# Cross-attention with a routed FFN on one core: scatters spread over half slots, x and result laid out by group and token, the last layernorm and the blocks' weights moved in the ending

## The chip, the cores and the metric

The kernel runs on one core of a Trainium2 chip. The metric is device time in microseconds for one launch. The engines are PE (TensorE), ACT (ScalarE), DVE (VectorE), POOL (GpSimd) and SP (SyncE, which here only issues DMAs). Each engine works through its own instructions in order.

## The reference, cut to what matters

There are 64 batches of 128 tokens with 128 features, and 77 context rows of 96 features for each batch. Everything is fp32.

```python
x = x + xattn(layernorm(x), ctx)       # 16 heads of 64, softmax over 77 keys, w_out, b_out
x2 = layernorm(x)
logits = x2 @ router_w.T               # 8 experts
gate = logits of the 2 experts with the highest softmax(logits), 0 elsewhere
moe = sum_e gate[:, e] * ((silu(x2 @ w1[e].T) * (x2 @ w3[e].T)) @ w2[e].T)      # I = 176
moe = moe + (silu(x2 @ sw1.T) * (x2 @ sw3.T)) @ sw2.T                          # shared expert
return x + moe
```

## The kernel before, in words

**Groups, units, half slots.** The batches are cut into 16 groups of four (G = 4). An attention unit is one batch with half of the heads, so there are 128 units, eight to a group. The main loop (lines 1075 to 1092) walks the units; each has two half slots, `run(2k)` and `run(2k+1)`, at which steps of a plan are called. A group thus has 16 half slots, group g starts at half slot 16 g, and `end` is 256. The plan is a dictionary written by `at(when, steps)` (lines 841 to 956). Each step puts its instructions behind those already there on each engine; the framework then places the instructions and their waits, and the order on POOL in particular can differ a little from the order of the plan.

**Attention.** Queries are never formed: keys times folded weights (pk, L334, copied to kx by ACT, L341) meet the transposed x (ps, L351). DVE subtracts the maximum (sc, L362), ACT takes exp (L366), DVE sums and inverts (ri, L375), POOL scales (tile `at`, L381 to L385, two buffers), PE transposes (pa, L420), ACT copies (aT, L423), PE multiplies with folded values (py, L430; the values are pv, L403, copied to vo by ACT, L408), and DVE adds to the residual x1 (L431). The group's inputs are loaded by SP two groups ahead (`load_inputs`, x at L111).

**Layernorm and router.** In the next group's half slots the finished group is normalised: DVE takes the statistics, POOL computes rs (L279), DVE the shift (L287), ACT writes the normalised rows into `pay` (L291, one buffer), PE transposes them (pxT, L304), ACT copies to x2T (L305), PE computes the logits, DVE chooses two experts and finds each token's row. `send(c, b)` (L632) is an indirect DMA on POOL (L635): it scatters the 128 rows of batch b for choice c, each with its destination and its gate, into a DRAM buffer `sent`, sorted by expert. There are eight sends to a group, and `pay` can be written again when the eight have been done.

**Blocks.** The groups form three sets (9, 5 and 2 groups). When the rows of a set are sent, `tables` (L675) turns the counts into a table of blocks of 128 rows of one expert. A `Quad` is four such blocks: `load` (L736, SP) reads the rows, `weights` (L758) copies the four experts' weights within SBUF, two by ACT and two by DVE, `transpose` (L764, L766), `first` and `rest` (L771) make the hidden rows in two parts, `down` (L783, L784) multiplies with w2, ACT scales by the gate into y (L791, two buffers), and `answer(j)` (L793) is an indirect DMA on POOL (L795), four to a quad, that scatters the results to a DRAM buffer by token. Set 0 has 20 quads, spread over the attention of set 1's groups; set 1 has 12, of which seven run every two half slots over the last attention and five (KEPT) in the ending.

**Combining.** `Combine` reloads a group's residual (L818) and its answers (L821), adds (L830), and stores the result (L834). For all groups but the last two the residual had been parked in DRAM.

**The ending.** After the last unit, a list of jobs (the kept quads, the two remaining shared experts, and the last set's quads) is run in a software pipeline (`ending`, L1020 to L1035). `ahead_of[k]` holds the steps that are issued before job k's `first`, `within[k]` those behind it. The last group's layernorm is split: batches 0 to 2 (`most_of`) are normalised in the last half slots of the plan, batch 3 (`rest_of`) at the start of the ending. The quads' copies of weights stand in `ahead_of`, two jobs early.

The places that the change touches:

```python
nc.sync.dma_start(out=xg, in_=x[bs].rearrange("b t d -> t b d"))                       # L111
at(p + 9 + k, lambda g=g, c=c, b=k: routers[g].send(c, b))                             # L926
at(p + 5 + j // 2, lambda quad=quad, j=j: quad.answer(j))                              # L950
at(end - 1, last("transpose", most_of), last("logits", most_of))                       # L990
0: [last("stats", rest_of), last("normed", rest_of)],                                  # L993
ahead_of.setdefault(max(k - 2, 5 if k > KEPT + 1 else 0), []).append(job["weights"])   # L1003
```

Of the kernel before, what the change touches and what calls it, by code (L numbers as in the profile page):

```python
# [8 lines left out]
F32 = mybir.dt.float32  # L9
# [6 lines left out]
B, NQ, D = 64, 128, 128  # L16
# [15 lines left out]
G = 4  # L32
NG = B // G
# [3 lines left out]
KEPT = 5  # L37
# [23 lines left out]
def xattn_moe_kernel(  # L61
# [17 lines left out]
    nc = tc.nc  # L79
# [26 lines left out]
    def load_inputs(g):  # L106
        bs = slice(g * G, (g + 1) * G)
        cT = grp.tile([DC, G, NKV], F32, tag="cT", name=f"cT_{g}", bufs=2)
        nc.sync.dma_start(out=cT, in_=ctxT[:, bs, :])
        xg = grp.tile([128, G, D], F32, tag="xg", name=f"xg_{g}", bufs=2)  # L110
        nc.sync.dma_start(out=xg, in_=x[bs].rearrange("b t d -> t b d"))  # L111
        return xg, cT

    def load_first_keys(g):
# [12 lines left out]
    def load_last_keys(g):  # L127
# [3 lines left out]
        return cR  # L131

    inputs, transposed = {0: load_inputs(0)}, {0: load_transposed(0)}
    first_keys, last_keys = {0: load_first_keys(0)}, {0: load_last_keys(0)}
    for q in range(2):
# [11 lines left out]
    def load_expert(e):  # L147
        nc.sync.dma_start(out=wx_sb[:, e, :], in_=wx[e * 128 : (e + 1) * 128, :])
# [11 lines left out]
    for i in range(NAT):  # L160
        a = const.tile([128, 8 * (KM + KS)], F32, name=f"at_{i}")
# [643 lines left out]
    class Combine:  # L805
# [24 lines left out]
                nc.vector.tensor_tensor(self.x1, self.x1, self.answers[:, c], ALU.add)  # L830

        def store(self):
            g = self.g
            self.queue.dma_start(out=out[g * G : (g + 1) * G].rearrange("b t d -> t b d"), in_=self.x1)  # L834

# [3 lines left out]
    def at(when, *steps):  # L841
        plan.setdefault(when, []).extend(steps)

    atts = {}
    routers = {}
# [26 lines left out]
    def load_group(g):  # L872
        inputs[g] = load_inputs(g)
# [10 lines left out]
    for g in range(NG):  # L884
        p = 16 * g
# [15 lines left out]
    def route(g, step, *args):  # L901
        if g not in routers:
            routers[g] = Router(g, next(s for s in sets if s.start <= g < s.start + s.n), atts[g].x1)
        getattr(routers[g], step)(*args)

    def routing(g, p, *steps):
        for k, step in steps:
            at(p + k, lambda step=step: route(g, step))

    g = 0  # L910
# [4 lines left out]
    for g in range(NG - 1):  # L915
        p = 16 * (g + 1)
        routing(g, p, (0, "stats"), (1, "normed"), (3, "transpose"), (3, "twice"), (4, "logits"), (4, "exps"), (5, "choose"), (6, "choose_second"))
    for st in sets:
        for g in range(st.start, min(st.start + st.n, NG - 1)):
            p = 16 * (g + 1)  # L920
            routing(g, p, (8, "place"))
            if g < NG - 2:
                routing(g, p, (11, "shared_up"), (12, "shared_rest"), (14, "shared_down"), (17, "park"))
            for k in range(4):
                for c in range(2):
                    at(p + 9 + k, lambda g=g, c=c, b=k: routers[g].send(c, b))  # L926
    end = 16 * NG
    for st in sets[:-1]:
        p = 16 * (st.start + st.n)
# [2 lines left out]
        st.ready = p + 16  # L932
    for g in range(2, 2 + E):
        at(16 * g + 8, lambda e=g - 2: load_expert(e))
    kept = []
    for st, after in zip(sets, sets[1:]):
        quads = [Quad(st, q) for q in range(st.quads)]
        until = after.ready - 16 if after is not sets[-1] else end - 4
        if after is sets[-1]:
            quads, kept = quads[:-KEPT], quads[-KEPT:]  # L940
        for q, quad in enumerate(quads):
            p = st.ready + (until - st.ready) * q // (len(quads) - 1)
            at(p - 3, quad.load)
            at(p - 1, quad.weights)
            at(p, quad.transpose)
            at(p + 1, quad.first)
            at(p + 2, quad.rest)
            at(p + 4, quad.down)
            for j in range(QUAD):
                at(p + 5 + j // 2, lambda quad=quad, j=j: quad.answer(j))  # L950
        if after is not sets[-1]:
            for j in range(st.n):
                c = Combine(st, j)
                at(p + 7 + 2 * j, c.load)
                at(p + 9 + 2 * j, c.add)
                at(p + 10 + 2 * j, c.store)
# [16 lines left out]
    def last(step, *args):  # L973
        return lambda: route(NG - 1, step, *args)
# [3 lines left out]
    def shared(g):  # L978
        return {
            "first": lambda: route(g, "shared_up", True),  # L980
            "rest": lambda: route(g, "shared_rest", True),
            "down": lambda: route(g, "shared_down"),
        }

    jobs = blocks[:3] + [shared(NG - 2)] + blocks[3:KEPT] + [shared(NG - 1)] + blocks[KEPT:]

    most_of, rest_of = range(G - 1), range(G - 1, G)
    at(end - 3, last("stats", most_of))
    at(end - 2, last("normed", most_of))
    at(end - 1, last("transpose", most_of), last("logits", most_of))  # L990

    ahead_of = {
        0: [last("stats", rest_of), last("normed", rest_of)],  # L993
        1: [last("choose"), last("choose_second")],
        2: [last("place"), last("twice")] + [last("send", c, b) for b in range(G) for c in range(2)],
        4: [lambda: tables(last_set)],
    }

    within = {0: [last("transpose", rest_of), last("logits", rest_of), last("exps")]}
    for k, job in enumerate(jobs):  # L1000

        if k and "weights" in job:
            ahead_of.setdefault(max(k - 2, 5 if k > KEPT + 1 else 0), []).append(job["weights"])  # L1003

    def ahead(k, step):
        ahead_of.setdefault(k, []).append(step)
# [1 line left out]
    for j in range(before_last.n):  # L1008
        c = Combine(before_last, j)
        k = KEPT + 3 + j  # L1010
# [3 lines left out]
    for j, queue in zip(range(last_set.n), (nc.sync, nc.scalar)):  # L1014
        c = Combine(last_set, j, queue, routers)
# [4 lines left out]
    def ending():  # L1020
        def do(k, step):
            if 0 <= k < len(jobs):
                jobs[k].get(step, lambda: None)()

        for k in range(max(ahead_of) + 1):
            do(k + 2, "load")
            for step in ahead_of.get(k, ()):
                step()
            do(k, "first")
            for step in within.get(k, ()):  # L1030
                step()
            do(k + 1, "transpose")
            do(k, "rest")
            do(k - 1, "down")
            do(k - 1, "answer")  # L1035
# [3 lines left out]
    at(end - 2, jobs[0]["weights"])  # L1039
    at(end - 1, jobs[0]["transpose"])  # L1040
    at(end + 2, ending)

    def run(when):
# [3 lines left out]
    def unit(k):  # L1047
        g, b, t = units[k]
        return attention_of(g), b, t
# [25 lines left out]
    for k in range(len(units) + 1):  # L1075
# [3 lines left out]
        if k and k % 2 == 0:  # L1079
            a, b, t = unit(k - 1)  # L1080
# [4 lines left out]
        a, b, t = unit(k)  # L1085
# [11 lines left out]
    last = {}  # L1097
# [12 lines left out]
def _laid_out(inputs):  # L1110

    import numpy as np

    a = {k: np.asarray(v) for k, v in inputs.items()}
    f = np.float32

    def packed(w1, w3, w2):

        w = np.zeros((128, WALL), f)
        w[:, W1:W3] = w1[:128].T  # L1120
        w[:, W3:WR] = w3[:128].T
        w[:, WR : WR + IR] = w1[128:].T
        w[:, WR + 64 : W2F] = w3[128:].T
        w[:, W2F:W2R] = w2[:, :128].T
        w[:IR, W2R:] = w2[:, 128:].T
        return w

    keys = a["ctx_768"].transpose(2, 0, 1)
    ctxR = np.zeros((DC, B, KS), f)
    ctxR[:, :, :KR] = keys[:, :, KM:]  # L1130
    ctxM = keys[:, :, :KM].reshape(DC, B // 2, 2 * KM)
    ctxM = np.concatenate([ctxM, ctxM[:, :, :KM]], axis=2)

    def by_pair(w):

        return w.reshape(NH // 2, 128, -1).transpose(1, 0, 2)

    w1, w2, w3 = (a[f"L0_ffn_w{n}"] for n in (1, 2, 3))
    return {
        "x": a["x"],  # L1140
        "xT": a["x"].transpose(2, 0, 1),
        "ctxT": keys,
        "ctxM": ctxM,
        "ctxR": ctxR,
        "wqT": by_pair(a["L0_xattn_w_q"].T),
        "wkT": by_pair(a["L0_xattn_w_kv"][:, :INNER].T),
        "wvT": by_pair(a["L0_xattn_w_kv"][:, INNER:].T),
        "w_out": by_pair(a["L0_xattn_w_out"]),
        "b_out": a["L0_xattn_b_out"],
        "rwT": a["L0_ffn_router_w"].T,  # L1150
        "wx": np.concatenate([packed(w1[e], w3[e], w2[e]) for e in range(E)]),
        "wsh": packed(a["L0_ffn_sw1"], a["L0_ffn_sw3"], a["L0_ffn_sw2"]),
    }
# [19 lines left out]
```

## Time and profile before

| | |
|---|---|
| time, median of 3 runs | 1010.59 us (1010.37 to 1012.74) |
| profiled execution, its own time | 1054.01 us |
| its span | 1052.3 us |
| its mean granted TensorE clock | 0.956 |
| PE busy | 945.9 us, 90% |
| DVE busy | 677.8 us, 64% |
| ACT busy | 653.7 us, 62% |
| POOL busy | 521.1 us, 50% |
| sends (L635) | 128 of 992 ns |
| answers (L795) | 152 of 986 ns |
| DMA packets | 81410, of them 63392 of 512 B to 2 KB |

The profile is of one execution, which took longer than the runs that were timed without it. A busy PE is not a PE at its peak, and busy shares are means over very different stages: the attention of the first nine groups, the attention with blocks between its units, and the ending. A row of the timeline has the start, the duration, the engine, the line, the operation, what is written from what, and how often; the brackets give the engine's idle time before it and what ended it. The suffix `_f` is the layernorm ahead of the FFN, `_a` that ahead of the attention.

### The profile page before, as it was taken

To read this page: it belongs to the slowest core of one execution; us is meant where nothing else is said; L and a number is where in the kernel's file an instruction comes from. 1 tells how busy PE (TensorE), PEld (TensorE's weight loads), DVE (VectorE), ACT (ScalarE), POOL (GpSimd) and SP (SyncE) were. 2 spreads that over 40 slices of the span, in tenths; PEclk is the share of its full clock that TensorE was granted. 3 is DMA by queue.
4 is the path that set the end of the run, shared out by engine and by line. 5 is a ranking of instruction groups with operands and counts; after the bars stand their busy time and mean duration, and the time that the engine had idled before them with its cause. 6 is when DMAs were issued, how large, how long until landed. Compare 5 with 4: busy or idle time off the path is not lost. (4 is left out here: it accounts for less than half of the span.)

```text
span 1052.3 us, 18905 instructions
## 1 busy us (share of the span) xinstructions
PE 945.9 (90%) x6136; PEld 785.1 (75%) x6136; DVE 677.8 (64%) x1773; ACT 653.7 (62%) x1421; POOL 521.1 (50%) x692
## 2 busy tenths in 40 slices
PE   7999999999999999999899898799999887666781
PEld 6887887878787787868787687698787676564781
DVE  4667767676676677786676567466758778334342
ACT  4777767667676766757667557557676475433550
POOL 3345363653536456353645555553656426626353
PEclk9999999999999999999999899999999899878896
DMA  5212122122212311233123122222212653211364
GB/s 169 75 39 79 57 62 79 56 72 76 76 40 63 99 55 55 83 85 88 47 77 91 56 67 60 60 66 84 64 57 90 195 169 108 64 28 58 89 199 138
DMA packets 81410, 86.16 MB, mean 82 GB/s; under 512 B 11424, under 2 KB 63392, under 8 KB 81312
## 3 DMA queue, kind: packets, MB, share of 16 engines
q1 hardware_dynamic: 66352, 56.29, 19.3%
q0 software_dynamic: 8960, 18.50, 5.3%
q10 hardware_dynamic: 6000, 10.16, 2.7%
q8 instruction: 49, 0.80, 0.3%
q14 instruction: 49, 0.40, 0.1%
HBM read 48.38 MB, written 36.53 MB: 81 GB/s over the span
## 5 line engine op out<-in xcount | busy, mean ns | idle before, releaser
L334 PEld LDWEIGHTS pk<-cT,wkq_sb 96*128 96x128 f32 x1024 | 159.4, 191 | 71.3 <-issue 47.9
L795 POOL DMA_INDIRECT answers<-y,to x152 | 149.9, 986 | 114.9 <-ACT y L791 52.7
L341 ACT COPY kx<-pk 128x308 f32<-128x308 f32 x256 | 104.1, 416 | 145.1 <-PE pk L334 103.9
L334 PE MATMUL pk<-cT,wkq_sb 96*128 96x154 f32 x1024 | 177.1, 297 | 1.3 <-DVE wkq_sb L246 1.3
L351 PE MATMUL ps<-kx,xgT 128*128 128x308 f32 x512 | 161.7, 437 | 10.1 <-DVE sc L362 9.5
L430 PEld LDWEIGHTS py<-vo,aT 128*128 128x128 f32 x1280 | 158.5, 197 | 15.4 <-ACT vo L408 2.7
L430 PE MATMUL py<-vo,aT 128*128 128x128 f32 x1280 | 160.7, 281 | 3.7 <-ACT aT L423 2.3
L383 POOL TENSOR_TENSOR at<-sc,ri 128x512 f32<-128x512 f32 x64 | 67.1, 1049 | 192.2 <-DVE ri L375 148.1
L635 POOL DMA_INDIRECT sent<-pay,row x128 | 126.9, 992 | 62.6 <-DVE part L625 29.4
L408 ACT COPY vo<-pv 64x512 f32<-64x512 f32 x256 | 147.0, 574 | 3.0 <-remote 0.7
L403 PE MATMUL pv<-wvo_sb,cM 96*128 96x512 f32 x256 | 131.5, 595 | 3.0 <-DVE hr L505 1.2
L373 DVE TENSOR_REDUCE sm<-sc 128x8 f32<-128x616 f32 x128 | 101.2, 790 | 39.6 <-ACT sc L366 38.7
L366 ACT ACTIVATE sc<-sc,rs_a 128x616 f32<-128x616 f32 x128 | 104.8, 819 | 31.1 <-DVE sc L362 30.2
L423 ACT COPY aT<-pa 128x512 f32<-128x512 f32 (+1 forms) x256 | 96.2, 429 | 42.3 <-PE pa L420 25.8
L351 PEld LDWEIGHTS ps<-kx,xgT 128*128 128x128 f32 x512 | 91.2, 194 | 38.5 <-issue 9.5
L381 POOL TENSOR_TENSOR at<-sc,ri 128x256 f32<-128x256 f32 x128 | 76.6, 621 | 87.1 <-DVE ri L375 41.8
L362 DVE TENSOR_TENSOR sc<-ps,mx 128x616 f32<-128x616 f32 x128 | 102.4, 800 | 12.6 <-POOL at L383 0.5
L360 DVE TENSOR_REDUCE mx<-ps 128x8 f32<-128x616 f32 x128 | 98.4, 768 | 8.7 <-PE ps L351 7.0
L420 PE MATMUL pa<-ident,at 128*128 128x128 f32 x640 | 92.0, 274 | 2.2 <-DVE lg L546 1.3
L771 PE MATMUL p<-xT,w 128*128 128x128 f32 x608 | 76.8, 280 | 14.0 <-ACT xT L766 7.3
L771 PEld LDWEIGHTS p<-xT,w 128*128 128x128 f32 x608 | 72.9, 196 | 18.2 <-ACT xT L766 9.3
L420 PEld LDWEIGHTS pa<-ident,at 128*128 128x128 f32 x640 | 75.2, 142 | 13.4 <-issue 11.8
(147 smaller groups left out, 1430.6 us busy)
## 6 DMA issues: line engine op xcount, KB each, us to landing
xb<-sent SPq DMA_DIRECT2D x152, 65.0 KB
last_values<-vn ACTq DMA_DIRECT2D x32, 256.0 KB
vo<-last_values SPq DMA_DIRECT2D x64, 128.0 KB
ya<-answers SPq DMA_DIRECT2D x15, 512.0 KB
xg<-in_x_dram SPq DMA_DIRECT2D x16, 256.0 KB
xgT<-in_xT_dram SPq DMA_DIRECT2D x16, 256.0 KB
parked<-x SPq DMA_DIRECT2D x14, 256.0 KB
ya<-parked SPq DMA_DIRECT2D x14, 256.0 KB
```

Source lines behind the costliest of these rows:

```text
L334: nc.tensor.matmul(pk[:, k].rearrange("p (b k) -> p b k", k=NKV), wkq_sb[:, 2 * i + k, :], self.cT[:, 2 * p : 2 * (p + 1), :], start=True, ...
L341: nc.scalar.copy(self.kx[p][:, hs, :], pk)
L351: nc.tensor.matmul(ps[:, r, : 4 * NKV].rearrange("p (j k) -> p j k", k=NKV), self.xgT[:, ts], self.kx[p][:, h : h + 4, ks], start=True, st ...
L362: nc.vector.tensor_tensor(at, sc, over_keys(mx), ALU.subtract)
L366: nc.scalar.activation(at, at, AF.Exp, scale=self.norm.rs[:, b : b + 1])
L403: nc.tensor.matmul(pv, self.cM[:, p, KM * r : KM * (r + 2)], wvo_sb[:, h : h + 4, :], start=True, stop=True)
L408: nc.scalar.copy(self.vo[b][rows, 4 * t : 4 * (t + 1), :], pv[rows].rearrange("p (m d) -> p m d", d=D))
L420: nc.tensor.transpose(pa[:, j * NQ : (j + 1) * NQ], keys[:, c : c + 128], ident)
L430: nc.tensor.matmul(py[:, :D], aT[:, m, :], vo[:, m, :], start=(m == 0), stop=(m == NT - 1))
L635: ins = nc.gpsimd.indirect_dma_start(out=sent[st.i], out_offset=bass.IndirectOffsetOnAxis(ap=self.row[:, i : i + 1], axis=0), in_=self.pay ...
L771: nc.tensor.matmul(to[:m, ts], self.w[j][:, c : c + m], self.xT[:, ts], start=True, stop=True)
L795: ins = nc.gpsimd.indirect_dma_start(out=answers[st.i], out_offset=bass.IndirectOffsetOnAxis(ap=self.to[:, j : j + 1], axis=0), in_=self.y ...
```

## The change

Five things are changed:

- **Layout.** The host lays x out as group, token, batch in the group, feature, and the output is written so and put back by the host. A partition's part of a group's x load and of its store is one run of 2 KB; before it was four runs of 512 B.
- **Sends.** The eight sends of a group stood two to a half slot, at p+9 to p+12. Now they stand one to a half slot, at p+9 to p+16, but for the last group of each set, which keeps two.
- **Answers.** The four answers of a quad stood two to a half slot, at p+5 and p+6. Now they stand one to a half slot, at p+5 to p+8, but for quads that start within the last seven half slots.
- **The last batch's layernorm.** Statistics and scaling of batch 3 of the last group stood at the start of the ending (half slot end+2, behind answers of the plan's last quads). They now stand at half slot `end`, and are entered in the plan ahead of the quads' steps. Transpose and logits of the other three batches move from end-1 to the start of the ending.
- **Weights.** In the ending a quad's copies of weights stood ahead of an earlier job's `first`. They now stand behind the transpose of the next job, ahead of the same job's `rest`.

```diff
-        nc.sync.dma_start(out=xg, in_=x[bs].rearrange("b t d -> t b d"))
+        nc.sync.dma_start(out=xg, in_=x[g])
...
-            self.queue.dma_start(out=out[g * G : (g + 1) * G].rearrange("b t d -> t b d"), in_=self.x1)
+            self.queue.dma_start(out=out[self.g], in_=self.x1)
...
-                    at(p + 9 + k, lambda g=g, c=c, b=k: routers[g].send(c, b))
+                    when = k if g == st.start + st.n - 1 else 2 * k + c
+                    at(p + 9 + when, lambda g=g, c=c, b=k: routers[g].send(c, b))
...
+    most_of, rest_of = range(G - 1), range(G - 1, G)
+    at(end, lambda: route(NG - 1, "stats", rest_of), lambda: route(NG - 1, "normed", rest_of))
     kept = []
...
-                at(p + 5 + j // 2, lambda quad=quad, j=j: quad.answer(j))
+                at(p + 5 + (j // 2 if p > end - 8 else j), lambda quad=quad, j=j: quad.answer(j))
...
-    at(end - 1, last("transpose", most_of), last("logits", most_of))
...
-        0: [last("stats", rest_of), last("normed", rest_of)],
+        0: [last("transpose", most_of), last("logits", most_of)],
...
+    behind = {}
...
-            ahead_of.setdefault(max(k - 2, 5 if k > KEPT + 1 else 0), []).append(job["weights"])
+            behind.setdefault(max(k - 2, 5 if k > KEPT + 1 else 0), []).append(job["weights"])
...
             do(k + 1, "transpose")
+            for step in behind.get(k, ()):
+                step()
             do(k, "rest")
...
-        "x": a["x"],
+        "x": a["x"].reshape(NG, G, NQ, D).transpose(0, 2, 1, 3),
```

More of the change, by code (lines that the diff above doesn't have):

```diff
@@ L832, in store @@
         def store(self):
-            g = self.g
-            self.queue.dma_start(out=out[g * G : (g + 1) * G].rearrange("b t d -> t b d"), in_=self.x1)
+            self.queue.dma_start(out=out[self.g], in_=self.x1)
     units = [(g, b, t) for g in range(NG) for b in range(G) for t in range(2)]
@@ L985, in xattn_moe_kernel @@
     jobs = blocks[:3] + [shared(NG - 2)] + blocks[3:KEPT] + [shared(NG - 1)] + blocks[KEPT:]
-    most_of, rest_of = range(G - 1), range(G - 1, G)
     at(end - 3, last("stats", most_of))
     at(end - 2, last("normed", most_of))
-    at(end - 1, last("transpose", most_of), last("logits", most_of))
     ahead_of = {
-        0: [last("stats", rest_of), last("normed", rest_of)],
+        0: [last("transpose", most_of), last("logits", most_of)],
         1: [last("choose"), last("choose_second")],
@@ L1167 @@
         args.append(nc.dram_tensor(f"in_{name}_dram", v.shape, mybir.dt.from_np(v.dtype), kind="ExternalInput").ap())
-    out = nc.dram_tensor("out_0_dram", (B, NQ, D), F32, kind="ExternalOutput").ap()
+    out = nc.dram_tensor("out_0_dram", (NG, NQ, G, D), F32, kind="ExternalOutput").ap()
     with _tile.TileContext(nc) as tc:
@@ L1171 @@
     r = _run(nc, [arrays], core_ids=[0])
-    return r.results[0]["out_0_dram"]
+    y = _np.asarray(r.results[0]["out_0_dram"]).reshape(NG, NQ, G, D)
+    return _np.ascontiguousarray(y.transpose(0, 2, 1, 3)).reshape(B, NQ, D)
```

## The prediction

> **What bounds the kernel now.** The page's first rows give TensorE 90% of the span, so I asked where the missing tenth lies, by a table of busy time in stretches (columns: stretch, its length, then busy microseconds and instruction counts of PE, weight loads, DVE, ACT, POOL, then the granted clock, the DMA share and GB/s).
>
> ```profile
> 254.60:344.40 89.80, 89.65 (x553) 71.57 (x552) 63.69 (x181) 62.31 (x136) 45.60 (x63) 1.00 0.23 68
> 860.00:930.00 70.00, 52.92 (x370) 47.19 (x368) 39.74 (x101) 36.10 (x84) 39.23 (x44) 0.90 0.28 78
> 1024.00:1052.00 28.00, 5.02 (x27) 4.34 (x26) 7.06 (x12) 2.48 (x9) 11.94 (x12) 0.63 0.47 149
> ```
>
> The first row is two groups of the attention phase (about 40 to 460): PE has 0.15 us of idle in 89.8. Nothing done on another engine can win time there; whatever makes PE wait is lost whole. The second row is the last attention, where expert blocks run between the units: PE rests 17 of 70 us, so chains of waits set the time. The third is the end, in which PE hardly works.
>
> Next I asked whether the softmax weights on POOL (tile at), which sends and answers sit between, hold PE up at all (columns: who waited, at what; us in total, times):
>
> ```profile
> who waited for it (us, times):
>   POOL at L383: 31.2, 7
>   ACT aT L423: 25.8, 28
>   ACT kx L341: 5.0, 1
>   PEld pa L420: 1.5, 1
> ```
>
> PE waits for it once, for 1.5 us. POOL itself sat idle 189.9 us before this tile for DVE's ri: it is early, not late. So spreading sends and answers out can win at most some 1.5 us directly.
>
> **The sum's base.** The profiled execution took 1054.01 us (span 1052.3 and 1.7 around it), 43.4 us over the median of 1010.59. Its timeline has stretches where engines stand with nothing waited for (958 to 980, 592 to 598, 893 to 900 and others, 37 to 40 us in my count), which I take to be most of that. I work out differences against the profiled execution and carry them over to the median one to one.
>
> **Sends, one to a half slot.** In the built order of the changed kernel, everything ahead of the ending is unchanged on PE, ACT, DVE and SP; only POOL's order moves. For groups 0 to 7 the eighth send of a group now stands directly behind rs of the next group's layernorm (L279). ACT's next step is pay (L291), which has one buffer and so waits for all eight sends of the group before; PE's transposes pxT (L304) wait for pay. Before:
>
> ```profile
> 293.18 1.04 POOL L279 TENSOR_TENSOR rs_f<-ve_f,mhalf 128x4 f32<-128x4 f32 x1 [2.33 <-DVE ve_f L278]
> ...
> 295.36 1.65 ACT L291 ACTIVATE pay<-x,shift_f,rs_f 128x128 f32<-128x128 f32 x4
> ...
> 297.31 0.60 PE L304 MATMUL pxT_f<-ident,pay 128*128 128x128 f32 x4
> ```
>
> rs ends at 294.22, pay ends at 297.01, PE begins 0.30 later. With the send in between: it starts at 294.37 (0.15 behind rs). How long until its receipt is not shown for a send; the nearest row is the last answer, issued at 1038.55 and read from 1040.79, 2.24 us (another pair gave 2.62). The Trainium skill ("DMA: Bandwidth & Descriptors", section "Anatomy of one DMA — SWDGE (gpsimd) path") gives about 2.0 us fixed, mostly the write receipt, and warns of longer delays when HBM is the target. By the page pay would start at 296.4, 1.0 late; by the rows at 296.6 to 297.0, 1.25 to 1.65 late. I take the rows: 1.35 us of PE stall in each of the four odd groups. In the even ones PE arrives 1.16 us behind pay's end (340.32 to 341.48), some 0.9 more slack, so 0.4 each. Sum 4 x 1.35 + 4 x 0.4 = 7.0. Bounds: 3 if ACT's vo copies, already between rs and pay, cover more of it; 14 if receipts take 3 us. It cannot be a gain, with PE full. For groups 9 to 12 PE has about 4 us between pay and pxT; ACT's own delay, some 2 us once, makes about +1 with the answers of the first set, whose y have 2.8 us or more of room (-1.5 to +3, the smoothing's 1.5 being the gain side).
>
> **Answers, one to a half slot.** In 860 to 930 the blocks come every two half slots, and y has two buffers: y of block q+2 waits for the last answer of block q. Before (the first two rows: last answer of block 0, then y of block 2):
>
> ```profile
> 872.14 1.01 POOL L795 DMA_INDIRECT answers<-y,to  x1
> ...
> 878.91 1.14 ACT L791 ACTIVATE y<-pq,xb 128x128 f32<-128x128 f32 x4 [3.17 <-PE pt L764]
> 880.19 0.30 PE L420 MATMUL pa<-ident,at 128*128 128x128 f32 x1 [0.88 <-ACT y L791]
> 880.74 1.04 POOL L383 TENSOR_TENSOR at<-sc,ri 128x512 f32<-128x512 f32 x1 [2.70 <-DVE ri L375]
> ```
>
> In the changed order that answer stands behind the at of 880.74, which with its rest (L385) ends at 882.13. It starts at 882.27, has landed at 884.5, and y begins 5.6 us later than 878.91; PE's pa at 880.19 already waited for y, so PE loses it too. What is queued on ACT behind y is aT, kx and exp. The same shape repeats: y of block 3 must wait for the answer behind the next at (ends 898.28 before, lands 899.6 or so against 888.28 before: +11.3), block 4 +9, block 5 +16.7, block 6 +11.8 (940.3 against 928.47). These do not add: each is the delay reached at that place, part of it soaked up by standing stretches of the profile.
>
> **The layernorm in front.** Before:
>
> ```profile
> 928.47 1.14 ACT L791 ACTIVATE y<-pq,xb 128x128 f32<-128x128 f32 x4 [4.67 <-PE pq L784]
> 929.11 0.96 POOL L795 DMA_INDIRECT answers<-y,to  x1 [5.94 <-ACT y L791]
> ...
> 932.90 0.97 POOL L795 DMA_INDIRECT answers<-y,to  x1 [0.30 <-issue]
> 933.89 0.58 POOL L279 TENSOR_TENSOR rs_f<-ve_f,mhalf 128x1 f32<-128x1 f32 x1
> 934.50 0.16 DVE L287 SCALAR_TENSOR_TENSOR shift_f<-mv_f,rs_f 128x1 f32<-128x1 f32 x1 [6.68 <-POOL rs_f L279]
> ```
>
> rs for the last batch, ready from 927.82, queued behind y of block 6 and its four answers for 6 us; shift, pay, one transpose, the logits and the router follow. In the changed order rs stands in front of them: 5.5 us saved on this chain. Its cost elsewhere is one rs of 0.58 on POOL, a shift of 0.16 on DVE and a pay of 0.49 on ACT ahead of y, all beside PE work. Against the delay above, the chain arrives at +6.7 at gsc and +8.8 at sel, the router's choice. **Together with the answers: +9**, from -5 (the y waits cost nothing) to +17 (no gain survives).
>
> **Layout.** Sixteen x loads and sixteen stores fall from four runs of 512 B per partition to one of 2 KB: 16,384 packets become 4,096. The Trainium skill ("Perfetto Trace Analysis", section "DMA Optimizations") says DMAs under 2 KB carry significant overhead per transfer, which would speak for a gain on all 32: with the last stores' 4.0 us (1048.2 to 1052.3) less about 2.2 of receipt, 1.8 us is movement, and three quarters of it 32 times would be 43 us. The rows speak against that: x is loaded two groups ahead with the DMA at a share of 0.23, and early stores have nobody behind them. Only the end is on the path: the last pair, about -1.3, and the combines in front of it (reload waits for store, 4.0 us once by SP's waits in 1000 to 1052), about -1. I take -2 (0 to -4).
>
> **Weights behind.** The copies of a block (ACT 1.33, DVE 0.88 for two) no longer stand ahead of a block's first half but behind the next transpose, ahead of its rest. No copy is added. In 980 to 1012 PE is busy 31.77 of 32 us, so nothing moves there; from 1024 twelve answers at 1.26 us set the pace. Only 935 to 958 can gain; a copy that comes late holds the next block's first half. -1 (-3 to +2).
>
> **Sum.** +7 +1 +9 -2 -1 = +14, say +13 as some delay will fall into stretches that already stand: 1010.6 + 13 = 1023.5 us.
>
> **Rivals.**
> - *The front position wins.* Place: rs at 928 to 934; price: -5.5 us. If y's waits for its answers fall into PE's 17 idle us of 860 to 930, the chain keeps the whole gain: with pay's stall at its low end, +3, the layout -2 and the weights -1, -5.5 in all, 1005. It decides once pay and y together cost less than the 8.5 that these three give. For it: PE is busy only 52.9 of 70 us there. Against: the 880.19 row shows PE waiting for y itself.
> - *Only pay stalls.* The y waits vanish, pay costs its 7: 7 + 1 - 5.5 - 2 - 1 = about 0, 1010.
> - *Receipts are slow.* If an indirect DMA takes 3 us or more beside other traffic (an answer at 1028.16 was waited for until 1033.37), pay costs 14 and the block chain 17: 14 + 1 + 17 - 3 = +29, some 1037 to 1040.
> - *The change doesn't reach the engines*: spoken against by the built order, in which sends, answers and rs do stand at new places.
>
> **How the numbers follow.** Main case 0.58 (1015 to 1032), slow receipts 0.15, front position wins 0.18, only pay stalls 0.09. A measurement of this kernel can tell about 0.3% (3 us) from no change. Faster by more: 0.19; within: 0.09; slower: 0.72, the first two cases less a little. For the range I reach down to 1003, over the winning case, and up to 1036, leaving out the worst receipts and the luckiest tail.
>
> **What would show it.** Right: pay in 90 to 460 waits for DMA ahead of eight groups, PE idle in 254 to 344 grows from 0.15 to about 3 us, the group pair from 89.8 to about 91.6; y in 860 to 940 ends its idle time on answers; rs for the last batch stands in front of the answers; the last stores take under 3 us. Wrong: PE full in 254 to 344 as before (then sends land early or POOL runs ahead), y not waiting for DMA, or a gain in 460 to 860, where I see none.

## The result, and the profile after

The changed kernel takes 1046.99 us (1043.03 to 1049.91, 4 runs) against 1010.48 (1009.28 to 1012.74): ratio 1.0356, 95% interval 1.0315 to 1.0397, or +36.5 us. Measured again beside the kernel before it was 1.0343 (1.0314 to 1.0372). I had forecast +13, with 1036 as the upper end: the direction held, my size was about a third of the measured one.

The profiled execution of the changed kernel took 1045.55 us, span 1043.8. The first profile of the kernel before (1054.01 us), which I had to reason from, is of a longer execution than a second one, from e1, with a span of 1010.6 us, which is "before" from here on; in the comparisons e9 to e12 and g1, g2 the kernel before took 1050 to 1052 us, and each of these is read only against the kernel before of its own comparison unless said otherwise.

To compare equal work I cut both spans at PE's transposes pxT: those of groups 1, 8 and 14, and the end. Both have, but for a record or two, the same matmuls in each stage. (Columns: stretch, length, busy us and counts of PE, weight loads, DVE, ACT, POOL, granted clock, DMA share, GB/s.) Before, second profile:

```profile
117.81:431.51 313.70, 313.15 (x1925) 250.27 (x1924) 223.71 (x637) 217.87 (x468) 159.89 (x217) 1.00 0.22 66
431.51:825.14 393.63, 377.20 (x2563) 319.66 (x2562) 285.44 (x712) 269.76 (x591) 216.78 (x263) 0.99 0.29 86
825.14:1010.60 185.46, 131.22 (x974) 118.59 (x972) 101.46 (x243) 88.22 (x199) 97.67 (x106) 0.87 0.39 116
```

After:

```profile
116.89:441.93 325.04, 317.58 (x1925) 250.61 (x1924) 223.60 (x636) 219.30 (x472) 161.35 (x218) 1.00 0.21 64
441.93:844.51 402.58, 379.25 (x2562) 322.59 (x2563) 281.44 (x712) 269.52 (x592) 215.69 (x263) 0.98 0.29 85
844.51:1043.80 199.29, 139.12 (x974) 126.58 (x972) 100.42 (x243) 89.06 (x199) 96.87 (x106) 0.83 0.35 107
```

The stages are 11.3, 9.0 and 13.8 us longer. Only part of that is idle time of PE (length less busy): 0.6 to 7.5, 16.4 to 23.3, 54.2 to 60.2, so +6.9, +6.9 and +6.0. The rest is PE being busy longer over the same matmuls: +4.4, +2.1 and +7.9. In the first stage, at a clock of 1.00, 3.0 of the 4.4 are in the transposes pxT alone (4.2 us busy before, 7.2 after), which wait within their row, as shown below; in the last the granted clock falls from 0.87 to 0.83. How the last stage splits is not the same in each execution: a second profile of the changed kernel (f1) has +10.0 idle and +5.6 busy there instead of +6.0 and +7.9. Over the whole execution PE's busy sum is 946.8 us against 933.3, PE's idle time 97.0 against 77.3.

What ACT waited for (columns: who, at what; us in total, times, longest), after:

```profile
ACT y L791 <- DMA answers<-y,to: 44.9, 7, 8.7
ACT pay L291 <- DMA sent<-pay,row: 11.8, 3, 6.0
```

Before, the only such row of the two:

```profile
ACT y L791 <- DMA answers<-y,to: 19.6, 4, 8.1
```

y already waited for its answers before the change; the profile that I predicted from has one such wait, of 7.0 us, in the ending (y at 1033.37). The wait of pay is new. The three places of the prediction, in the timeline of after. The first is a boundary between groups:

```profile
298.45 1.04 POOL L279 TENSOR_TENSOR rs_f<-ve_f,mhalf 128x4 f32<-128x4 f32 x1 [2.32 <-DVE ve_f L278]
...
299.69 1.06 POOL L635 DMA_INDIRECT sent<-pay,row  x1 [0.20 <-issue]
302.16 1.65 ACT L291 ACTIVATE pay<-x,shift_f,rs_f 128x128 f32<-128x128 f32 x4 [1.43 <-DVE sc L362]
...
302.71 1.49 PE L304 MATMUL pxT_f<-ident,pay 128*128 128x128 f32 x4
```

The send stands between rs and pay, and pay begins 2.47 us behind the send's start. The row blames DVE's sc, which ended 0.04 us earlier; but pay reads nothing of sc, and before the change it began ahead of that sc. What it waits for is the eight sends: 2.47 us is the same landing as in the rows below that name the DMA. rs ends at 299.49, so pay stands 2.67 us behind it where it stood 1.14 behind before; PE then takes the transposes one by one as ACT delivers them (1.49 us where it was 0.60). The second place is the blocks:

```profile
876.23 1.04 POOL L383 TENSOR_TENSOR at<-sc,ri 128x512 f32<-128x512 f32 x1 [3.72 <-PE pa L420]
...
877.76 1.01 POOL L795 DMA_INDIRECT answers<-y,to  x1
...
880.22 1.14 ACT L791 ACTIVATE y<-pq,xb 128x128 f32<-128x128 f32 x4 [8.75 <-DMA answers<-y,to]
...
882.34 3.46 PE L771 MATMUL p<-xT,w 128*128 128x128 f32 x16 [3.21 <-ACT xT L766]
```

The fourth answer stands behind `at`, y begins 2.46 us after that answer's start, and PE waits for xT, which ACT has queued behind y. The sixteen matmuls that follow take 3.46 us; the same sixteen took 1.95 before where PE came to them without a wait. The third place I had not seen:

```profile
926.02 0.96 POOL L635 DMA_INDIRECT sent<-pay,row  x1 [0.30 <-issue]
...
928.51 1.26 ACT L291 ACTIVATE pay<-x,shift_f,rs_f 128x128 f32<-128x128 f32 x3 [6.05 <-DMA sent<-pay,row]
...
931.51 2.93 PE L430 MATMUL py<-vo,aT 128*128 128x128 f32 x12 [11.80 <-ACT aT L423]
...
935.59 0.58 POOL L279 TENSOR_TENSOR rs_f<-ve_f,mhalf 128x1 f32<-128x1 f32 x1 [6.09 <-DVE ve_f L278]
```

The last group's pay waits 6.05 us for group 14's eighth send, which sits on POOL behind answers; aT is queued on ACT behind pay, and PE stands 11.8 us (e6 below takes this place out of the kernel with the sends alone and gets 10 us back). Only then can py finish the last batch, and rs, now ahead of the answers, has to wait for DVE instead.

### The profile page after: what moved, and what is told of

Same layout as the page of the kernel before. It is cut to its first block, busy times and chain, and to the rows that moved or that the text cites. A ratio compares the mean times of both kernels' runs of the same rounds, so it can differ in the third digit from the quotient of the medians.

```text
span 1043.8 us, 18864 instructions
## 1 busy us (share of the span) xinstructions
PE 946.8 (91%) x6136; PEld 787.7 (75%) x6136; DVE 677.9 (65%) x1773; ACT 654.7 (63%) x1421; POOL 522.3 (50%) x692
## 5 line engine op out<-in xcount | busy, mean ns | idle before, releaser
L334 PEld LDWEIGHTS pk<-cT,wkq_sb 96*128 96x128 f32 x1024 | 158.0, 190 | 69.9 <-issue 45.7
L430 PE MATMUL py<-vo,aT 128*128 128x128 f32 x1280 | 159.7, 280 | 16.7 <-ACT aT L423 11.8
L351 PE MATMUL ps<-kx,xgT 128*128 128x308 f32 x512 | 156.8, 427 | 10.0 <-DVE sc L362 9.4
L635 POOL DMA_INDIRECT sent<-pay,row x128 | 129.1, 1008 | 56.0 <-DVE part L625 26.0
L351 PEld LDWEIGHTS ps<-kx,xgT 128*128 128x128 f32 x512 | 88.8, 189 | 37.0 <-DVE sc L362 7.9
L771 PE MATMUL p<-xT,w 128*128 128x128 f32 x608 | 85.9, 301 | 20.2 <-ACT xT L766 19.4
L771 PEld LDWEIGHTS p<-xT,w 128*128 128x128 f32 x608 | 81.3, 215 | 25.0 <-ACT xT L766 23.0
```

The source lines that it names most:

```text
L334: nc.tensor.matmul(pk[:, k].rearrange("p (b k) -> p b k", k=NKV), wkq_sb[:, 2 * i + k, :], self.cT[:, 2 * p : 2 * (p + 1), :], start=True, ...
L351: nc.tensor.matmul(ps[:, r, : 4 * NKV].rearrange("p (j k) -> p j k", k=NKV), self.xgT[:, ts], self.kx[p][:, h : h + 4, ks], start=True, st ...
L430: nc.tensor.matmul(py[:, :D], aT[:, m, :], vo[:, m, :], start=(m == 0), stop=(m == NT - 1))
L635: ins = nc.gpsimd.indirect_dma_start(out=sent[st.i], out_offset=bass.IndirectOffsetOnAxis(ap=self.row[:, i : i + 1], axis=0), in_=self.pay ...
L771: nc.tensor.matmul(to[:m, ts], self.w[j][:, c : c + m], self.xT[:, ts], start=True, stop=True)
```

## The experiments

All were made of the kernel before with parts of the diff; where nothing else is said the whole of the reference is computed. Times are medians beside the kernel before of the same comparison.

**e1: the kernel before again.** No edit.

> The kernel before, unchanged, to have a profile of it without the standing stretches of the first one. Every theory expects 1010.5 us, ratio 1.000, and PE full from 85 to 444 us. If the standing stretches (about 40 us with nothing waited for) belong to the profiled execution alone, the span here is near 1009 us; if they belong to the kernel, it is again near 1050.

1011.36 us, ratio 1.0006 (0.9990 to 1.0022); span 1010.6. The standing stretches of the first profile are no fixed part of this kernel; what brings them is not shown.

**e2: sends alone.**

```diff
-                    at(p + 9 + k, ...
+                    when = k if g == st.start + st.n - 1 else 2 * k + c
+                    at(p + 9 + when, ...
```

> The kernel before with the sends alone spread out. Theory 1 (ACT stands at pay until the eighth send has landed, and PE with it): the eight group boundaries of 85 to 444 cost 11 us together, as in the changed kernel, and the last group's pay (L291) waits for the last send of the group before it, another 5 to 10 us: 1025 to 1032 us in all. Rival (the answers alone carry the loss of the last attention): 1021 to 1022, that is only the 11 us of the group boundaries.

1036.89 us, ratio 1.0265 (1.0227 to 1.0303), +26: theory 1's mechanism, and the largest part of the whole, some 5 us above theory 1's range. In its trace the first stage is 11.7 us longer, the second 4.5, and the last 8.1, with ACT standing 10.8 us at the last group's pay and PE 13.6 at pxT. Its stages two and three:

```profile
442.57:840.73 398.16, 376.28 (x2561) 318.51 (x2562) 283.42 (x712) 270.31 (x592) 216.33 (x263) 0.99 0.29 85
840.73:1034.30 193.57, 131.32 (x974) 119.09 (x972) 99.95 (x243) 88.46 (x199) 97.28 (x106) 0.86 0.37 110
```

PE's busy time is about that of before in both (376.3 and 131.3 against 377.2 and 131.2): here the loss is idle time.

**e3: answers alone.**

```diff
-                at(p + 5 + j // 2, ...
+                at(p + 5 + (j // 2 if p > end - 8 else j), ...
```

> The kernel before with the answers alone spread out. Theory 1 (each y waits for the fourth answer of the block two before, four times in a row, and the delay adds up round by round): 1022 to 1030 us, with ACT y waiting for DMA answers by 7 to 9 us at each of four y in 860 to 930. Rival (PE's idle time in 860 to 930 soaks the waits up, and the pay wait carries the loss there): 1010 to 1014.

1015.87 us, ratio 1.0052 (1.0035 to 1.0069), +5. Between the two theories: two y of the last attention wait for a fourth answer, not four in a row. One row says so (8.0 us); of the other, y at 862.23 us, it blames PE, but y begins 2.46 us behind an answer issued at 859.77, behind `at`, as in the changed kernel. From block to block the delay stays at 5 to 8 us (blocks 2 to 6: 7.0, 6.8, 4.9, 8.4, 5.0) rather than growing.

**e4: layout alone** (the first two and the last hunk of the diff).

> The kernel before with the layout of x and of the result alone. Theory 1: the x loads are hidden and only the last stores count: 1007 to 1010.5 us. Rival (2 KB runs to and from one partition load the DMA engines unevenly and delay what shares them): above 1013.

1010.16 us, ratio 1.0000 (0.9981 to 1.0019): nothing, either way. The packets fell as they should (each count takes in the smaller ones, so that before the 63392 were all packets under 2 KB, not those of 512 B to 2 KB):

```profile
DMA packets 69122, 86.16 MB, mean 85 GB/s; under 512 B 11424, under 2 KB 47008, under 8 KB 69024
```

From the last store's issue to the end it is 3.9 us (1005.04 to 1008.9), against 4.1 before (1006.53 to 1010.6).

**e5: sends alone, but the eighth in the half slot of the seventh.**

```diff
-                    when = k if g == st.start + st.n - 1 else 2 * k + c
+                    when = k if g == st.start + st.n - 1 else min(2 * k + c, 6)
```

> The kernel before with the sends alone spread out, but the eighth put into the half slot of the seventh, ahead of rs of the next layernorm rather than behind it. Theory 1 (only the place of the eighth send, between rs and pay, costs time in 85 to 444): the 12 us that the eight group boundaries cost in the run of the sends alone are gone; what the last group's pay costs may stay: 1011 to 1020. Rival (spread sends cost time wherever they end, by making POOL late for the softmax weights): 1030 or more, little less than the 1036.9 of the sends alone.

1011.39 us, ratio 1.0005 (0.9992 to 1.0019). All 26 us hang on the place of one send in eight. PE is full again in the attention phase:

```profile
254.60:344.40 89.80, 89.65 (x550) 71.58 (x550) 63.69 (x181) 62.30 (x135) 45.64 (x62) 1.00 0.23 68
```

The same seven sends spread over the same half slots win nothing either, as PE's waits for POOL said (the list in the prediction goes on with two more weight loads that waited, 1.4 and 0.5 us).

**e6: sends alone, but group 14 as before.**

```diff
-                    when = k if g == st.start + st.n - 1 else 2 * k + c
+                    when = k if g in (st.start + st.n - 1, NG - 2) else 2 * k + c
```

> The kernel before with the sends alone spread out, but those of group 14 kept two to a half slot. Theory 1 (the last group's pay waits for the eighth send of group 14, which stands behind 12 answers): PE's wait for pay near 911 falls from 13.6 back to about 6 us, and 6 to 8 us of the 26 are gone: 1028 to 1031. Rival (that wait is covered by the blocks around it): 1035 to 1038.

1026.95 us, ratio 1.0155 (1.0129 to 1.0180): 10 us of the 26 are group 14's alone, somewhat more than the 6 to 8 expected. PE's wait for pay is back at 6.2 us.

**e7: layernorm in front alone** (`most_of` and `rest_of` moved up, the step at `end`, the step at `end - 1` taken out, and `ahead_of[0]`).

> The kernel before with the last batch's layernorm alone moved ahead of the answers (and the transposes and logits of the other three batches with it). Theory of the prediction: rs stands no longer behind four answers, -5.5 us, 1005. Rival (rs in front waits for DVE's statistics and ACT's pay stands in front of y, or the moved transposes hold the first block's hidden rows): no gain, 1010 to 1016.

1002.36 us, ratio 0.9914 (0.9891 to 0.9937), -8.9: the one part that gains, and more than the 5.5 of the prediction. In the timeline, e7:

```profile
895.67 0.58 POOL L279 TENSOR_TENSOR rs_f<-ve_f,mhalf 128x1 f32<-128x1 f32 x1 [2.18 <-DVE ve_f L278]
...
897.04 1.14 ACT L791 ACTIVATE y<-pq,xb 128x128 f32<-128x128 f32 x4
```

and before:

```profile
900.71 1.14 ACT L791 ACTIVATE y<-pq,xb 128x128 f32<-128x128 f32 x4 [5.12 <-PE pq L784]
...
906.12 0.59 POOL L279 TENSOR_TENSOR rs_f<-ve_f,mhalf 128x1 f32<-128x1 f32 x1
```

rs comes 10.4 us earlier: 5.4 of queueing behind y and its answers (900.71 to 906.12), and the rest since y itself comes 3.7 earlier and rs stands ahead of it by 1.4; the transposes and logits of the other three batches no longer stand on PE between the last unit and py (894.76 before, 891.59 here). Its last stage:

```profile
824.68:1000.90 176.22, 126.89 (x974) 115.27 (x972) 101.45 (x243) 87.98 (x199) 98.15 (x106) 0.91 0.41 121
```

9.2 us shorter, of which 4.9 are idle time (54.2 to 49.3) and 4.3 are faster matmuls, at a granted clock of 0.91 against 0.87.

**e8: weights behind alone** (the `behind` hunks).

> The kernel before with the copies of weights alone moved behind the transposes. Theory of the prediction: -1 us, 1008 to 1011. Rival (the copies come late for the block two jobs on, or push xT and the hidden rows back on ACT and DVE): 1012 to 1018.

1010.20 us, ratio 1.0003 (0.9988 to 1.0018): nothing.

One by one the parts sum to 26 + 5 - 9 + 0 + 0 = +22. The whole is +36. The next comparisons ask where the other 14 are.

**e9 to e12**: the changed kernel without the sends, sends with answers, the changed kernel without the answers, and the changed kernel with the eighth send of e5.

> The changed kernel with the sends left as before. One by one the parts gave +26 (sends), +5 (answers), -9 (layernorm in front) and 0 (layout, weights), +22 together, where the whole change gives +36: 14 us more. Theory A (spread sends and spread answers delay each other on POOL) and theory B (the layernorm's gain is lost when the sends are late): -4, 1006 to 1009 us. Theory C (spread answers take the layernorm's gain away): 1016 to 1021.

> The kernel before with the sends and the answers spread out, nothing else. Theory A (they delay each other on POOL: sends stand behind answers, answers behind y, y behind older answers): the 14 us lie here, 1052 to 1058 us. Theories B and C (what is lost is the layernorm's gain, here absent): the plain sum, 1040 to 1044.

> The changed kernel with the answers left as before. Theory A: the plain sum of sends and layernorm, 26 - 9, 1026 to 1030 us. Theory B (spread sends hold the last group's pay and take the layernorm's gain away, and more): 1035 to 1045. Theory C: 1026 to 1030.

> The changed kernel with the one difference that the eighth send goes into the half slot of the seventh. If the place of the eighth send is the cause of all that the sends cost, also together with the answers: the sum of answers and layernorm, 1006 to 1010 us. If spread sends delay answers by their number on POOL wherever the eighth stands: 1016 to 1024.

Ratios 1.0086 (1.0065 to 1.0107), 1.0282 (1.0221 to 1.0344), 1.0025 (0.9994 to 1.0056) and 0.9953 (0.9929 to 0.9977), beside a kernel before of 1050.5 us. They say nothing of a sum of parts measured beside 1011 us: beside such a kernel before the first and the third gave 0.9992 and 1.0169 (f3 and f4 below). Why they differ is not shown. One thing holds within the comparison: with the eighth send one half slot earlier the otherwise changed kernel is faster than the kernel before. How much it would be beside 1011 us was not measured.

**f1 to f4**, the first three of these again beside the changed kernel, where the kernel before took 1011.0 us.

> The changed kernel itself, beside the kernel before on one chip. Every theory expects +36 us where the kernel before takes 1010 us; where it takes 1050 us (with its standing stretches) less, since waits fall into those.

> Sends and answers spread, nothing else, to be set against the changed kernel of the same chip. Theory A (they delay each other on POOL): 8 us or so over the changed kernel, whose layernorm in front gives its gain back, +43 to +46 over the kernel before. Theories B and C (the layernorm's gain is lost in the changed kernel): the plain sum of the two parts, +31, under the changed kernel.

> The changed kernel with the sends as before. Theories A and B: -4 against the kernel before. Theory C (spread answers take the layernorm's gain away, as the +9 of the last comparison says): +5 to +10 also here.

> The changed kernel with the answers as before. Theories A and C: sends 26 less layernorm 9, +17 against the kernel before. Theory B (spread sends take the layernorm's gain away): +26 or more.

| kernel | ratio (95% interval) | us | sum of parts |
|---|---|---|---|
| f1 changed kernel | 1.0343 (1.0314 to 1.0372) | +34 | +22 |
| f2 sends, answers | 1.0412 (1.0381 to 1.0443) | +42 | +31 |
| f3 all but sends | 0.9992 (0.9979 to 1.0005) | -1 | -4 |
| f4 all but answers | 1.0169 (1.0139 to 1.0200) | +16 | +17 |

Sends and answers together cost 11 us more than one by one: they act on each other, as theory A has it. Theory B falls (f4 is the plain sum). Theory C's 3 us are no more than the three intervals leave open. f2's stages two and three:

```profile
444.06:850.43 406.37, 383.23 (x2561) 325.07 (x2562) 281.77 (x712) 270.05 (x592) 215.73 (x263) 0.97 0.29 83
850.43:1056.70 206.27, 140.65 (x974) 127.37 (x972) 100.16 (x243) 87.96 (x199) 97.34 (x106) 0.81 0.35 104
```

The table has PE's busy and idle time in these two stages together, from pxT of group 8 to the end:

| profile | span | PE busy there | PE idle there |
|---|---|---|---|
| e1 before | 1010.6 | 508.4 | 70.7 |
| e4 layout | 1008.9 | 507.0 | 70.1 |
| e8 weights | 1010.0 | 507.9 | 69.9 |
| e5 sends, one half slot earlier | 1014.1 | 511.0 | 71.5 |
| e2 sends | 1034.3 | 507.6 | 84.1 |
| e6 sends, not group 14 | 1027.7 | 507.8 | 74.6 |
| e3 answers | 1017.0 | 509.0 | 75.1 |
| e7 layernorm | 1000.9 | 502.4 | 67.7 |
| f2 sends, answers | 1056.7 | 523.9 | 88.8 |
| f3 all but sends | 1007.8 | 504.2 | 70.4 |
| f4 all but answers | 1024.9 | 506.9 | 75.4 |
| after | 1043.8 | 518.4 | 83.5 |
| f1 after, again | 1046.9 | 517.0 | 86.0 |

Idle time in f2 is near the plain sum: 13.5 for the sends and 4.4 for the answers are 17.9, and f2 has 18.1 more than before. Busy time, of the same matmuls, is not: -0.8 and +0.5, but +15.5 together. How far to trust the split: kernels whose time did not change (e4, e5, e8) lie within 1.4 below and 2.6 above before; f2's profile is of the longest of its four runs (1058.42 us, median 1052.94); and f4 has some 5 us less idle and some 6 more busy time than its parts. So most of the 15.5 is beyond scatter, but not single microseconds.

Where it happens shows in one stretch, from pxT of group 14 to PE's wait for the last group's pay, with the same 392 matmuls in each. Before, sends (e2), answers (e3), both (f2):

```profile
825.14:883.40 58.26, 50.28 (x392) 44.91 (x390) 47.27 (x110) 34.50 (x79) 32.39 (x40) 1.00 0.45 126
840.73:898.00 57.27, 51.71 (x392) 46.56 (x390) 45.92 (x110) 34.20 (x76) 30.21 (x38) 0.97 0.42 124
826.15:887.70 61.55, 53.25 (x392) 47.12 (x390) 45.86 (x110) 33.76 (x76) 32.89 (x41) 0.92 0.39 114
850.43:924.70 74.27, 58.60 (x392) 52.63 (x390) 46.23 (x110) 33.76 (x76) 33.82 (x42) 0.84 0.34 98
```

Sends cost nothing here (-1.0), answers 3.3, both 16.0. Of the 16.0, 7.7 are idle time and 8.3 are longer matmuls. So theory A holds as it was told, as a longer wait: with the sends between them on POOL, the answers land later, and four y in a row (blocks 2 to 5) wait 7.7 to 8.5 us for them, where in e3 two wait. And it costs about as much again in slower matmuls, at a granted clock of 0.84. That idle time adds up over the whole of f2 is then partly luck: behind this stretch f2 loses 6.4 us less than the sum of its parts, PE's wait for pay being 11.2 us instead of e2's 13.6.

**g1 and g2: a third buffer for y**, its room from u (one buffer instead of two; four tiles that use u's room at the start move to that of h).

```diff
-            self.y = ffn.tile([128, QUAD, D], F32, tag="y", name=f"y_{self.name}")
+            self.y = ffn.tile([128, QUAD, D], F32, tag="y", name=f"y_{self.name}", bufs=3)
```

> Sends and answers spread, with a third buffer for y (its room comes from u, which gets one buffer instead of two; DVE alone writes and reads u). If the 15 us that the answers bring on top of the sends (42 against 26) come from y waiting for the answer of the block two before: 26 to 30 us over the kernel before, with ACT's four waits of some 8 us each for answers in 880 to 930 gone. If they come from sends standing behind answers on POOL, or from u: still 38 us or more.

> The kernel before with the layernorm in front (1002.4 us alone) and a third buffer for y. The three waits of y for answers in that run (4.5, 1.0 and 4.7 us) are gone; if PE was held by them: 994 to 1000 us. If they lie beside other waits: 1001 to 1004, no better than the layernorm alone.

Ratios 1.0129 (1.0083 to 1.0175) and 0.9937 (0.9920 to 0.9954), beside 1052.2 us. Against e10, the same orders with two buffers and a kernel before alike (1.0282 beside 1050.5 us), the third buffer takes 1.5% off, some 16 us, and y's waits for answers are gone from ACT's list. 13.6 us of it are in the stretch of the 392 matmuls, first e10, then g1:

```profile
852.86:929.00 76.14, 57.68 (x392) 51.27 (x390) 45.80 (x110) 33.82 (x76) 34.27 (x42) 0.84 0.31 91
858.95:921.50 62.55, 51.95 (x392) 46.44 (x390) 46.14 (x110) 34.31 (x76) 33.95 (x42) 0.97 0.39 111
```

With y's waits the slower matmuls go too: 5.7 us of busy time, and the clock is 0.97 again. So what answers and sends make together in this stretch is y's wait for older answers. What is left is the sends' (ACT waits 12.0 us for them at pay). The kernel before with a third buffer alone was not run; its stretch takes 58.26 us with two. Whether g2 beats e7 can't be told, as the two stood beside different times of the kernel before; e7's 1002.4 us is the best of both kernels' parts that was measured beside 1011.

## Why the prediction was wrong

Right: the direction, the three mechanisms (pay behind the eighth send, y behind the fourth answer, rs in front), that spreading wins nothing, and the landing of an indirect DMA (2.47 and 2.46 us where I took 2.24 to 2.62). y's delays place by place came out near, partly by luck. Against before, and less the 19.4 us by which after is late at group 14, y of blocks 2 to 6 comes 6.7, 11.0, 14.6, 18.7 and 17.3 us late; I had 5.6, 11.3, 9, 16.7 and 11.8. But I had worked these out for the answers, and the answers alone (e3) delay y by 5 to 8 us only; the growing delay comes with the sends. (For block 3 my own landing of 2.24 us gives 12.4, not 11.3.)

What failed is seen best by parts. Sends: +7 and +1, measured +26 (e2). All the rest: 9 - 2 - 1 = +6, measured -1 (f3, 0.9979 to 1.0005). The two together: no term, measured about 10 more (f1's +34 against 25). By stages of the changed kernel:

- **The sends at the group boundaries: +7, measured +11.3.** Pay is 1.5 us later behind rs, inside my 1.25 to 1.65. But I charged PE only with pay's delay. What ACT has behind pay came late as well: in e2 PE waits eight times for vo at py (4.9 us) and four times for kx ahead of pxT (2.4 us), rows that before has once (1.6 us) or not. The term was mis-sized, inside its bounds of 3 to 14.
- **Behind group 8, up to group 14: +1, measured +9.0.** The sends make 4.5 of it (pay waits 3.0 us for them at one group), the answers alone none (-0.4 in e3). The rest comes only with both; of f2's 12.7 us in this stage 6.0 are longer busy time.
- **The last stage: +9 for answers with layernorm, and -2 and -1 for layout and weights; measured +13.8.** I followed the sends only to group 12; group 14's eighth send holds the last group's pay, which e6 prices at 10 us and I had at nothing. Without the sends my +9 is not there: answers +5 and layernorm -9 are -4, and f3 has -1. The layernorm's own -5.5 was too small (-8.9), and the answers' delay, which I let eat it up, is small without the sends between them. The layout and weights gave nothing: stores that nobody waits for, at 3.9 instead of 4.1 us for the last where I had taken 1.3 off, and copies that moved beside other waits.
- **No term for the clock.** My +14 was a sum of waits. Measured, the first stage's 11.3 us are idle time, drawn-out transposes and what hangs on them, and the idle time of the others is 6.9 and 6.0, about 24; the other 10 (2.1 and 7.9; in f1 3.0 and 5.6) are the same matmuls taking longer. Behind a wait of 3.21 us sixteen matmuls took 3.46 us instead of 1.95 (the granted clock was 0.50 from 881.90 to 885.31), and in e7 fewer waits bought 4.3 us of faster matmuls. The Trainium skill ("TensorE: Matmul & The Clock Gate", section "What's actually happening") says that PE falls to half its clock after an idle window of about 3.4 us, and returns after about as much sustained work. Half the clock is what the rows show, but shorter waits brought it on too, and not every time. e1 and e4 wait the same 1.65 us for sc (ps, L351, at 465.15 and 465.47); the next 3.41 us, e1 then e4, ran at 0.50 and at 1.00:

```profile
464.88:468.29 3.41, 3.14 (x8) 2.44 (x9) 3.25 (x7) 2.27 (x4) 3.19 (x5) 0.50 0.02 5
465.47:468.88 3.41, 3.41 (x24) 3.12 (x25) 3.25 (x6) 2.59 (x5) 3.19 (x5) 1.00 0.04 15
```

For the ramp, the time until the clock is full, the same section gives less than 1% of a typical kernel; but here the clock falls more than once, as waits come again every 12 to 14 us in the last attention, and the difference alone is 1.0% of the span, in f2 (6.0 and 9.4 us) 1.5%. My profile had shown a granted clock of 0.90 in 860 to 930, and I read past it.

Of the rivals, slow receipts came nearest in size (+29) for a wrong reason: the receipts that pay and y waited for, 2.3 to 2.5 us in the last attention, were as fast as I took them.

## What to carry to other kernels

When a step is spread over later slots, look at the last of its instructions and ask which single-buffer tile it frees, at every place where it happens, the last group too: one send in eight made all of 26 us, and one half slot undid it. Price a wait on a path that bounds PE with the matmuls behind it as well: in the last stage, where PE already rests, idle time came with half as much to rather more than as much slow-clock time (7.9 beside 6.0 and 5.6 beside 10.0 us in the two profiles of the changed kernel, 4.3 beside 4.9 the other way). Try the parts of a bundle one by one, and then in pairs; here one of five gained 0.9%, two did nothing, two lost, and those two, which share POOL, lost 11 us more together.

## What the runs showed of the hardware that I had not expected

The clock's cost does not add: in the stages behind group 8, sends and answers changed PE's busy time by -0.8 and +0.5 us alone and by +15.5 together, over the same matmuls. And it is not sure to come: after the same wait of 1.65 us the granted clock was 0.50 for 3.41 us in one profile and 1.00 in another. Kernels of the same time (e4, e5) differ by 4 us in PE's busy sum there. A quarter of the packets for x and the result (69122 in all instead of 81410) changed the time by nothing that could be measured (0.9981 to 1.0019).
